# Two of four sums of transposed probabilities: formed by VectorE instead of GpSimd

## The chip, the cores and the metric

The kernel runs on one core of one Trainium2 chip. Five engines work side by side, each with its own queue of instructions, and meet through semaphores: TensorE (PE in the profile, with PEld for its weight loads), VectorE (DVE), ScalarE (ACT), GpSimd (POOL) and SyncE (SP, which here only issues DMAs). The metric is the time of one execution on the device, in microseconds (us). Lower is better. All data are float32.

## The reference

`x` has 8 batches of 100 rows of 512; `ctx` has 8 batches of 361 rows of 512. A small cross-attention with one head comes first, then a block with two cross-attentions of 16 heads of 128 over the same context, and an MLP:

```python
q, k, v = x @ w_q.T, ctx @ w_k.T, ctx @ w_v.T
x = x + alpha * (softmax(q @ k.T / sqrt(512)) @ v) @ w_o.T

for i in (1, 2):                       # two layers, 16 heads, K = 128
    h = layer_norm(x) * ln_scale + ln_offset
    qh, kh, vh = h @ wq + bq, ctx @ wk + bk, ctx @ wv + bv     # by head
    kh, vh = concat(kh, bias_k), concat(vh, bias_v)            # one more key: 362
    w = softmax(qh @ kh.T / sqrt(128))
    x = x + (w @ vh) @ wo + bo
h = layer_norm(x) * ln_scale + ln_offset
x = x + gelu(h @ w_fc1 + b_fc1) @ w_fc2 + b_fc2
```

## The kernel before

The 8 batches are taken in four pairs: `q` numbers the pair and `j` the batch within it (`QB` = 2). `l` is the layer. The 16 heads of 100 rows of a batch make 1600 rows, and these are cut into three groups `g` (`ROWS`: 576, 512 and 512 rows). A step is one `(l, q, g)`, so that there are 24 steps with two batches each, 48 rounds in all.

Instead of forming keys and values, the kernel multiplies each query by the transposed key weight (`queries`, `wide_queries`) and puts the result into the large tile `Z`. The scores are then `Z` times the context, and after the softmax the probabilities times the context go back into the same place in `Z` (`mixed`), from where `head_out` applies the value weight.

Both products are done with a scheme of seven block products instead of eight, in the manner of Strassen and Winograd. Such a scheme needs sums and differences of the blocks of both operands:

- For the scores, `pair_sums` (L700 to L703, GpSimd) forms four sums of blocks of `Z` for two tiles of 128 rows. `pair_part` runs the seven products in four parts. L752, L757 and L758 on VectorE add what comes out in PSUM. `pair_exps` takes the row maximum (L770, VectorE) and the exponential (L771, ScalarE), and `rows_normed` divides by the sum (L337 on VectorE, L338 on ScalarE). L751 on GpSimd writes the score of the extra key into the tile of probabilities, for which the transposes of that tile's former contents must be done.
- For the second product the probabilities must have the keys on the partitions. `rows_turned` calls `turned`, which transposes blocks of 32 by 32 on VectorE (L354), 16 instructions for a pair of tiles and 8 for the single tile of 64 rows in group 0. They go into `pT`, a tile of nine blocks: 0 to 5 hold the transposed probabilities, 6, 7 and 8 take sums. After the last transpose of a round `column_sums` writes one row to DRAM (L790, a DMA issued by SyncE) and forms four sums, L791 to L794. In the text L791 is the first sum (block 6), L792 the one that overwrites block 1, L793 the second (block 7) and L794 the last (block 8).
- `mixed` then runs the seven products with the context for each half `m` of the columns. Its part 0 needs block 6, part 1 needs block 7, part 2 the new block 1 and part 3 block 8. Its results are copied or added into `Z` by ScalarE (L836, L839, L844, L858) and VectorE (L847, L853, L854).

Other VectorE work that the text speaks of: L577 scales the transposed rows of a layer norm, L884 adds the bias of a head's output, L946 and its neighbours add up the output projection, L595 multiplies weights for the score of the extra key, L458 to L460 form sums of the transposed context in the first small attention, and L986 to L995 are sums of the same kind in the MLP.

The order of the units is written out by hand at the end of the program: `score_units` gives the parts of the scores of one round, and the products of the round before (`mix_units`), the projections of the next step and the output heads are woven between them. Within this order a planner of the framework gives each engine its own order, by rank: an instruction's rank is its place in the program, and the transposes get a rank 30 places later (`TURN_BEHIND`), so that they yield to other VectorE work. The four sums have the rank of their place.

`column_sums` has an argument for the engine, which is GpSimd unless `last_turned` calls it with VectorE. `score_units` reuses the name `n` before `end` reads it, so that `last_turned` is never built: in the profile all 48 rounds have their four sums on GpSimd.

Of the kernel before, what the change touches and what calls it, by code (L numbers as in the profile page):

```python
# [11 lines left out]
ALU = mybir.AluOpType  # L12
# [67 lines left out]
def two_cross_attentions(ctx: ExitStack, tc: tile.TileContext, a: dict, out: bass.AP):  # L80
    nc = tc.nc
# [696 lines left out]
    def columns(l, q, g, j):  # L778

        r0, r1 = ROWS[g]  # L780
        if (l, q, g, j) not in pTs:
            t = work.tile([P, 9 * GWIDTH // 2], F32, tag="pT", name=f"pT_{l}_{q}_{g}_{j}")
            pTs[l, q, g, j] = t[:, : 9 * (r1 - r0) // 2].rearrange("p (u n) -> p u n", u=9)
        return pTs[l, q, g, j][:, :6, :].rearrange("p (k h) n -> p k (h n)", k=3)

    def column_sums(l, q, g, j, engine=nc.gpsimd):


        t, t3 = pTs[l, q, g, j], columns(l, q, g, j)
        nc.sync.dma_start(out=pbd[l, q * QB + j][:, slice(*ROWS[g])], in_=t3[TS : TS + 1, 2, :])  # L790
        engine.tensor_tensor(t[:, 6], t[:, 1], t[:, 0], ALU.subtract)  # L791
        engine.tensor_tensor(t[:, 1], t[:, 1], t[:, 3], ALU.subtract)  # L792
        engine.tensor_tensor(t[:, 7], t[:, 3], t[:, 6], ALU.subtract)  # L793
        engine.tensor_tensor(t[:, 8], t[:, 2], t[:, 7], ALU.subtract)  # L794

    def rows_turned(l, q, g, j, r, quarter):

        p, dens, rows = probs[l, q, j, r]
        n = rows * len(dens)
        c0 = r - ROWS[g][0]  # L800
        turned(p, columns(l, q, g, j)[:, :, c0 : c0 + n], len(dens), rows, quarter)
        if r + n == ROWS[g][1] and quarter == 3:
            column_sums(l, q, g, j)

    def last_turned(l, q, g, j, r, m):

        p, _, rows = probs[l, q, j, r]
        c0 = r - ROWS[g][0] + m * P
        transposed(f"{l}_{q}_{r}_{m}", p[:, m, :], rows, columns(l, q, g, j)[:, :, c0 : c0 + rows])
        if m:  # L810
            column_sums(l, q, g, j, nc.vector)
# [520 lines left out]
```

## Time and profile before

| | |
|---|---|
| median of 3 runs | 2040.84 us (2040.75 to 2043.89) |
| the profiled execution | 2040.29 us, of which the span from the first to the last instruction is 2038.2 |
| mean granted TensorE clock | 0.995 |
| VectorE, busy | 1282.4 us |
| GpSimd, busy | 702.0 us |
| L354, the transposes on VectorE | 1664 instructions, 602.0 us |
| L791 to L794, on GpSimd | 48 each, median 0.73 us each |

The profile comes from one execution. "Busy" is the time in which an engine ran at least one instruction. A row of a group of instructions gives, after the bar, the busy time in us and the mean time of one in ns, then after the next bar the idle time of the engine just ahead of these instructions and, behind `<-`, what ended most of it. A row of the list of waits reads: the engine and its instruction, `<-` what it waited for, then the total, the number of waits and the longest. A line of the timeline has the start, the duration, the engine, the line, what is written and read and, in brackets, the idle time before it. TensorE takes two passes for a float32 product, so that each product shows as two instructions.

### The profile page before, as it was taken

The page shows a single profiled execution, that of the slowest core. Times are in us where ns is not written, and L with a number is a line of the kernel's source. Part 1 is how long each engine was busy: PE and PEld are TensorE (multiplying, and loading weights), DVE is VectorE, ACT ScalarE, POOL GpSimd, SP SyncE. Part 2 cuts the span into 40 slices and gives each one's busy share as a digit, 9 for nine tenths or more (in the row PEclk, how much of TensorE's full clock was granted, in tenths as well). Part 3 has the DMA queues.
Part 4 walks back from the last instruction along what each step waited for, and adds up shares of the span by engine and source line. Part 5 has one row for each costly group of instructions (what it writes and reads, how often), then busy time and mean ns, then how long its engine had stood idle before and what let it go on. Part 6 is the DMA issues. An engine that isn't in the chain of part 4 may idle for free.

```text
span 2038.2 us, 31454 instructions
## 1 busy us (share of the span) xinstructions
PE 1974.1 (97%) x10991; PEld 1801.1 (88%) x10991; DVE 1282.4 (63%) x3523; ACT 760.0 (37%) x2002; POOL 702.0 (34%) x1146
## 2 busy tenths in 40 slices
PE   9999999999999999999999999999999999989998
PEld 5668889998989889998999998989998998979998
DVE  2564766667666676666775766676767666765543
ACT  1324444444442343444432444444433444421231
POOL 3232432643344143534234322333243244225140
PEclk9999999999999999999999999999999999999999
DMA  8696224742645445534634453234244432135342
GB/s 256 251 322 191 83 81 135 217 134 78 191 133 153 131 138 176 181 97 128 207 113 131 114 184 103 87 93 156 87 124 123 145 115 82 56 97 164 111 129 74
DMA packets 250681, 283.87 MB, mean 139 GB/s; under 512 B 37608, under 2 KB 212108, under 8 KB 247196
## 3 DMA queue, kind: packets, MB, share of 16 engines
q1 hardware_dynamic: 246340, 271.51, 43.0%
q0 software_dynamic: 2112, 6.40, 0.9%
q10 hardware_dynamic: 2072, 3.97, 0.6%
q8 instruction: 87, 1.43, 0.3%
q14 instruction: 70, 0.57, 0.1%
HBM read 242.86 MB, written 38.97 MB: 138 GB/s over the span
## 4 chain that ended last, share of the span: by engine, by line
PE 73%; DVE 13%; DMA 5%; ACT 4%; POOL 3%; issue 2%; SPq 0%; DVEq 0%; POOLq 0%; ACTq 0%
PE sx L717 9%; PE mx L827 8%; PE mz L827 7%; PE pwo_P L940 7%; PE pq L657 7%; DVE pT L354 6%; PE po L877 6%; PE pqw L673 6%; PE sz L717 4%; PE my L827 3%; PE sy L717 2%; PE pfx L1080 2%; DMA xr<-xd 2%; PE sc L470 2%; PE pgx L1031 2%
## 5 line engine op out<-in xcount | busy, mean ns | idle before, releaser
L354 DVE STREAM_TRANSPOSE pT<-p 32x192 f32<-32x192 f32 (+1 forms) x1664 | 602.0, 362 | 84.6 <-ACT p L338 55.4
L827 PE MATMUL mx<-pT,ctx 128*128 128x256 f32 (+3 forms) x960 | 282.8, 393 | 21.1 <-ACT Z L836 6.2
L717 PE MATMUL sx<-cT,Z 128*128 128x181 f32 x1152 | 230.9, 319 | 5.6 <-DVE p L757 4.2
L751 POOL TENSOR_SCALAR p<-nsb 128x1 f32<-128x1 f32 x192 | 37.4, 214 | 532.7 <-DVE pT L354 490.2
L827 PE MATMUL mz<-pT,ctx 105*128 105x256 f32 (+3 forms) x768 | 209.3, 395 | 11.0 <-POOL pT L791 10.5
L717 PEld LDWEIGHTS sx<-cT,Z 128*128 128x128 f32 x1152 | 195.6, 191 | 20.1 <-DVE p L757 6.9
L827 PEld LDWEIGHTS mx<-pT,ctx 128*128 128x128 f32 (+1 forms) x960 | 169.2, 190 | 44.3 <-POOL pT L793 9.2
L877 PE MATMUL po<-Z,wv 128*128 128x200 f32 x1024 | 193.9, 333 | 0.8 <-DMA wv<-in_L_xattn_wv_dram 0.8
L673 PE MATMUL pqw<-q,wkT 128*128 128x200 f32 x1024 | 194.6, 332 | 0.0
L657 PE MATMUL pq<-hT,wq 128*128 128x200 f32 x1024 | 193.6, 333 | 0.0
L771 ACT ACTIVATE p<-p,nm 128x362 f32<-128x362 f32 x192 | 114.8, 598 | 190.0 <-DVE nm L770 187.6
L827 PEld LDWEIGHTS mz<-pT,ctx 128*128 128x128 f32 (+1 forms) x768 | 145.2, 192 | 43.5 <-POOL pT L791 14.7
L673 PEld LDWEIGHTS pqw<-q,wkT 128*128 128x128 f32 x1024 | 176.3, 190 | 5.4 <-issue 0.5
L877 PEld LDWEIGHTS po<-Z,wv 128*128 128x128 f32 x1024 | 175.0, 189 | 6.4 <-issue 1.3
L657 PEld LDWEIGHTS pq<-hT,wq 128*128 128x128 f32 x1024 | 175.0, 189 | 4.2 <-issue 1.4
L770 DVE TENSOR_REDUCE nm<-p 128x1 f32<-128x362 f32 x192 | 101.5, 529 | 103.1 <-ACT p L762 93.2
L717 PE MATMUL sz<-cT,sums 128*128 128x181 f32 x768 | 149.4, 316 | 1.1 <-ACT p L745 1.1
L700 POOL TENSOR_TENSOR sums<-Z 128x256 f32<-128x256 f32 x96 | 69.7, 726 | 233.3 <-ACT Z L676 158.6
L676 ACT COPY Z<-pqw 128x400 f32<-128x400 f32 x256 | 122.4, 490 | 68.5 <-PE pqw L673 68.4
L338 ACT ACTIVATE p<-p,rden 128x362 f32<-128x362 f32 (+2 forms) x216 | 129.0, 599 | 36.9 <-DVE rden L337 36.9
L717 PEld LDWEIGHTS sz<-cT,sums 128*128 128x128 f32 x768 | 124.7, 189 | 1.7 <-ACT p L745 1.6
L827 PE MATMUL my<-pT,ctx 128*128 128x256 f32 (+3 forms) x384 | 102.9, 389 | 0.0
(377 smaller groups left out, 3115.7 us busy)
## 6 DMA issues: line engine op xcount, KB each, us to landing
wv<-in_L_xattn_wv_dram SPq DMA_DIRECT2D x64, 512.0 KB
wq<-in_L_xattn_wq_dram SPq DMA_DIRECT2D x64, 512.0 KB
wkT<-wkd SPq DMA_DIRECT2D x48, 512.0 KB
cT<-cTd SPq DMA_DIRECT2D x16, 1267.0 KB
wo_S<-wod SPq DMA_DIRECT2D x32, 512.0 KB
f<-in_L_xattn_w_fc_dram SPq DMA_DIRECT2D x32, 512.0 KB
wo_A<-in_L_xattn_wo_dram SPq DMA_DIRECT2D x24, 512.0 KB
xr<-xd SPq DMA_DIRECT2D x46, 200.0 KB
```

The costliest lines, as they stand in the source:

```text
L338: nc.scalar.mul(p[:rows, :n], p[:rows, :n], rden[:rows])
L354: nc.vector.transpose(dst[keys, :, :, i, :], src[i * QD : (i + 1) * QD, :, :, quarter, :])
L657: nc.tensor.matmul(ps, w[:, c, (h % 2) * K : (h % 2 + 1) * K], hTs[l, q][:, c, :], start=(c == 0), stop=(c == DT - 1),)
L673: nc.tensor.matmul(ps[:, c, :], w[:, h % 2, cc * P : (cc + 1) * P], qs[h], start=True, stop=True)
L676: nc.scalar.copy(Z[:, 2 * c2 : 2 * c2 + 2, :, h * L : (h + 1) * L], ps.rearrange("p c (b t) -> p c b t", b=QB),)
L700: nc.gpsimd.tensor_tensor(t[:, 0], a2[:, :2, :], a2[:, 2:, :], ALU.add)
L717: nc.tensor.matmul(ps[:, :KH], st["a"][a][:, c, :], st["ct"][:, blk, c, :], start=(first and c == 0), stop=(c == 1), skip_group_check=not ...
L770: nc.vector.tensor_reduce(nm, p[:, :S1], AX.X, ALU.max, negate=True)
L771: nc.scalar.activation(p[:, :S1], p[:, :S1], AF.Exp, bias=nm, accum_out=den)
L827: nc.tensor.matmul(ps, cx[:w, blk, :], pT[:w, u, :], start=first, stop=last, skip_group_check=more)
L877: nc.tensor.matmul(ps, w[:, c, (h % 2) * K : (h % 2 + 1) * K], Z[:, c, :, h * L : (h + 1) * L], start=(c == 0), stop=(c == DT - 1),)
L940: nc.tensor.matmul(ps, w[:, h, :], OB[i, j][:, h, :], start=(h == 0 and not more), stop=(h == 7), skip_group_check=more)
```

## The change

The first and the third instruction of `column_sums`, L791 and L793, are issued to VectorE. L792 and L794 stay on the engine that is passed in, GpSimd in all 48 rounds. The operands, their shapes and the order in the program stay.

```diff
         t, t3 = pTs[l, q, g, j], columns(l, q, g, j)
         nc.sync.dma_start(out=pbd[l, q * QB + j][:, slice(*ROWS[g])], in_=t3[TS : TS + 1, 2, :])
-        engine.tensor_tensor(t[:, 6], t[:, 1], t[:, 0], ALU.subtract)
+        nc.vector.tensor_tensor(t[:, 6], t[:, 1], t[:, 0], ALU.subtract)
         engine.tensor_tensor(t[:, 1], t[:, 1], t[:, 3], ALU.subtract)
-        engine.tensor_tensor(t[:, 7], t[:, 3], t[:, 6], ALU.subtract)
+        nc.vector.tensor_tensor(t[:, 7], t[:, 3], t[:, 6], ALU.subtract)
         engine.tensor_tensor(t[:, 8], t[:, 2], t[:, 7], ALU.subtract)
```

The second sum reads the first, now on the same engine. L792 overwrites block 1, which the first sum reads, and L794 reads the second sum; both now follow VectorE.

## The prediction

> **What bounds the kernel now.** I read the page's busy shares first, then TensorE's waits in the attention part, then single places in the timeline.
>
> ```profile
> PE 1974.1 (97%) x10991; PEld 1801.1 (88%) x10991; DVE 1282.4 (63%) x3523; ACT 760.0 (37%) x2002; POOL 702.0 (34%) x1146
> ```
>
> TensorE works 97% of the span: with the work on it unchanged, only its idle 64 us can be won. By stage, it idles 14.5 us before 205 us, 38.9 between 205 and 1830 (the attention layers, where every column sum lies) and 10.7 in the MLP. Next I asked what ended the 38.9; the columns are the total, the number of waits and the longest, in us:
>
> ```profile
> PE mz L827 <- POOL pT L791: 10.5, 10, 2.3
> PE mx L827 <- ACT Z L836: 6.2, 4, 2.7
> PE mx L827 <- DVE Z L853: 5.1, 6, 2.1
> PE mx L827 <- POOL pT L793: 4.9, 6, 0.9
> PE sx L717 <- DVE p L757: 3.4, 4, 2.2
> ```
>
> The first and the fourth wait are on the two sums that move: together 15.4 us, 0.75% of the time and the ceiling of the direct gain. The second, third and fifth show the other side: TensorE also waits on evictions by ScalarE and VectorE, and VectorE gets more to do. One place shows the whole mechanism (start, duration):
>
> ```profile
> 495.31 0.75 DVE L354 STREAM_TRANSPOSE pT<-p 32x192 f32<-32x192 f32 x2
> ...
> 496.14 0.72 POOL L791 TENSOR_TENSOR pT<-pT 128x256 f32<-128x256 f32 x1 [0.91 <-DVE pT L354]
> ...
> 496.92 0.73 PEld L827 LDWEIGHTS mz<-pT,ctx 128*128 128x128 f32 x4 [1.22 <-POOL pT L791]
> 496.92 1.13 PE L827 MATMUL mz<-pT,ctx 128*128 128x256 f32 x4 [0.82 <-POOL pT L791]
> ...
> 498.19 0.72 POOL L793 TENSOR_TENSOR pT<-pT 128x256 f32<-128x256 f32 x1
> ...
> 498.97 0.70 PE L827 MATMUL mx<-pT,ctx 128*128 128x256 f32 x2 [0.91 <-POOL pT L793]
> ```
>
> The last transposes end at T = 496.06. GpSimd starts 0.08 later, takes 0.72, and TensorE goes on 0.06 after it, 0.86 after T. Then the queue holds a pair sum (L700) and L792 ahead of L793, so the second wait follows. In 35 of the 48 places the first sum waits directly for its transposes like this; in the other 13 GpSimd was still on other work.
>
> **Prices.** From the groups kept apart by shape:
>
> ```profile
> L854 DVE TENSOR_TENSOR Z<-my,Z 128x256 f32<-128x256 f32 x64 | 26.9, 421 | 1.9 <-PE my L827 0.4
> L791 POOL TENSOR_TENSOR pT<-pT 128x256 f32<-128x256 f32 x32 | 23.3, 729 | 55.9 <-DVE pT L354 29.2 <-issue 26.7
> L793 POOL TENSOR_TENSOR pT<-pT 128x256 f32<-128x256 f32 x32 | 23.2, 727 | 0.0
> ```
>
> No VectorE row has this size with both inputs in SBUF. L854 (one input in PSUM) gives 421 ns, and 446 at 288 columns; a line through 569 ns at 400 columns (L989) and 1222 at 1024 (L992 to L995) gives 418. I take 0.42 and 0.45.
>
> **What the Trainium skill says.** GPSIMD Engine Reference, section Elementwise — side-by-side cycle accounting: a two-input sum is about twice as fast on VectorE, mostly per element. Here it is 0.42 against 0.73. SBUF — State Buffer, section SBUF: two separate sides: a VectorE operation with two SBUF inputs and a GpSimd operation that reads SBUF take one port pair as an exclusive lock, whoever starts first. The trace agrees:
>
> ```profile
> 97.75 0.74 DVE L458 TENSOR_TENSOR cT_-1_4_631<-cT_-1_4_631 128x362 f32<-128x362 f32 x1
> 98.53 0.94 DVE L459 TENSOR_TENSOR cT_-1_4_631<-cT_-1_4_631 128x362 f32<-128x362 f32 x1
> 99.40 1.05 DVE L460 TENSOR_TENSOR cT_-1_4_631<-cT_-1_4_631 128x362 f32<-128x362 f32 x1
> ```
>
> Beside GpSimd's context sums L460 takes 1.05; elsewhere 0.53. Perfetto Trace Analysis, section Tensor Engine Instruction: VectorE and GpSimd run strictly in order, so what counts is where the planner puts the moved sums.
>
> **Part by part.**
>
> *Removed from GpSimd:* 2 x 48 sums, 23.3 + 14.3 + 23.2 + 12.7 = 73.5 us busy. GpSimd is 34% busy, so this pays nothing by itself; what pays is which result comes sooner.
>
> *Added to VectorE:* 32 x 2 x 0.42 + 16 x 2 x 0.45 = 41.3 us, to about 65%. Their rank in the order is the normal one, the transposes' is 30 lower, so the first sum should be next as soon as the last transpose is out, and the second behind it. No new wait on VectorE for another engine: the first sum reads only what VectorE wrote, the second also the first (some 0.07 for the hand-over; L993 starts about that long after L992).
>
> *First sum ready:* T + 0.03 + 0.42 + 0.06 = T + 0.51, not T + 0.86. In the ten waits: at 298.5, 496.9, 927.8 and 1352.4 (0.82, 0.82, 1.03, 0.82) 0.35 each is won, 1.40; at 239.9 (0.55, 288 columns) 0.40; at 1817.3 (2.34) 0.41; at 722.7 (1.09), where GpSimd came 0.37 after T, 0.64; at 210.9, 833.5 and 1729.8 (1.03, 0.35, 1.69) GpSimd was busy with L700 to L703 for 0.8 to 2.6 us past T, and the whole wait goes, 3.07. Sum 5.9.
>
> *Second sum ready:* T + 0.94, or T + 1.67 behind one GpSimd operation holding the lock. In the place shown TensorE would want it at about T + 1.63, so all six waits go: 4.9. Gross gain 10.8.
>
> *Third and fourth sum stay on GpSimd:* L792 must not overwrite what the first sum reads, so GpSimd now waits for VectorE there, until T + 0.53, where it used to wait for the transposes until T + 0.08. Behind it are L794, L751 and the pair sums L700 to L703. But two operations of 0.73 have left the queue: L792 ends near T + 1.3 to 1.7 and L794 near T + 2.0 to 2.4; before, 2.2 and 3.0 without other work between. No wait of TensorE on either was recorded, and I expect none.
>
> *VectorE's hold:* 0.94 us in 48 places, 1.67 with one lock wait, 2.3 with two. What is queued behind: L752, L757, L758, L946, L577, L884 or the next softmax. For each place I subtracted VectorE's idle gaps before the next L757 or L853 and that one's slack to the matmul that waits for it (mostly 1.4 to 2.7). A hold of 0.94 then delays TensorE once, by 0.9 (at 760.4, slack 0.05); 1.67 costs 2.2 in four places; 2.3 costs 8.2 in twelve. At 760.4 VectorE is itself locked out by GpSimd's column sums, which become fewer, so 0.9 may vanish. I take 1.5; the bounds are 0 and 8.2. The scores' own chain (maximum, exponential, reciprocal, transposes) is covered by gaps of 0.8 to 2.3 us within the next few instructions.
>
> *DMA and queues:* nothing is moved. L790, issued by SyncE, reads the transposes and stays in front; no DMA is issued by VectorE or GpSimd here.
>
> *Given back:* TensorE arrives earlier at later waits. The ones on L836, L853 and L757 hang on engines that TensorE itself feeds and shift along; those on DMAs don't. I take 1.4 of the 10.8, a choice.
>
> Sum: 10.8 - 1.5 - 1.4 = 7.9. Profiled execution: 2038.2 span + 2.1 around it = 2040.3; the median is 2040.8, 0.5 above. So about 2032.4 for a profiled run and **2033 us** for the median. About 0.2%, 4 us, is what a measurement can tell from no change.
>
> **The rivals.**
>
> *The lock makes VectorE late (slower).* GpSimd wakes from L751 on the same transposes and starts L700 or L792 just then. If both new sums regularly wait a whole 0.73, the hold is 2.3 and costs 8.2; the first sum comes at T + 1.24, 0.4 later than now in seven of the ten waits (2.7 lost; 3.1 still won in the other three), and of the second's 4.9 about 2.5 remain. Net 8.2 + 2.7 - 3.1 - 2.5 = 5.3 slower: 2046. For it: the doubled L460, and L988 at 1.66 for 0.57. Against it: in 35 places GpSimd is idle until T, so VectorE starts first. It decides from a hold of about 1.8 us up, where the slacks of 1.4 to 1.8 are used up.
>
> *The gain is given back.* If what follows each removed wait is bound elsewhere (L836 and L853 come right after in the same product), three quarters are lost: 2.7 - 1.5, about 1 us faster, 2040. For it: 17% of the chain that ended last runs over VectorE and ScalarE. Against it: TensorE has only 39 us of idle left there.
>
> *Deeper gain.* With 73 us off GpSimd the pair sums come earlier, L595 meets fewer locks, and part of the waits on L853 and L836 goes as well: 5 more, and 2027.
>
> *The sums don't sit behind their block.* If the planner places them behind an eviction that waits for TensorE (L752 and L946 stand idle up to 2.3 us there), the first sum comes 1.5 to 3 us late in some places: up to 6 slower, 2047. The ranks speak against it.
>
> **How the numbers follow.** Chances: the forecast 0.55 (2029 to 2037), deeper 0.13, given back 0.15, lock 0.12, misplaced 0.05. Faster by over 0.2%: nearly all of the forecast, the deeper case and a little of the third, 0.67; within: most of given back and the forecast's edge, 0.16; slower 0.17. The range reaches from the deeper case to the lock: 2026 to 2045.
>
> **What would show it.** Right: waits of TensorE on L791 near 4.6 us, now under VectorE; those on L793 gone; L791 and L793 on VectorE at 0.42 to 0.6 mean; VectorE busy near 1325, GpSimd near 630; TensorE's idle in 205 to 1830 near 31. Wrong: means near 0.9 on VectorE (lock), or waits on L757, L853 and L836 grown by as much as those on L791 and L793 shrank.

## The result, and the profile after

| | before | after |
|---|---|---|
| median of five runs each | 2040.75 us (2038.72 to 2043.89) | 2048.60 us (2048.44 to 2051.75) |
| ratio | 1 | 1.0036, 95% interval 1.0021 to 1.005 |
| profiled execution, and its span | 2040.29, 2038.2 us | 2051.75, 2049.8 us |

The change makes the kernel slower, by 7.8 us in the medians and 7.3 by the ratio. The prediction, 2033 and a range of 2026 to 2045, missed the sign. The profiled execution of after is the longest of its five, 3.2 us above the next, so its page shows 11.6 us of span where the medians show 7.8.

The page's line of busy shares, after:

```profile
PE 1977.6 (96%) x10991; PEld 1806.6 (88%) x10991; DVE 1326.4 (65%) x3619; ACT 758.2 (37%) x2002; POOL 640.8 (31%) x1050
```

The work went where it was to go: VectorE has 44 us more, GpSimd 61 less. Of the 11.6 us of span TensorE's idle time has 8.1 (2049.8 - 1977.6 against 2038.2 - 1974.1) and its busy time, for the same instructions, 3.5. TensorE idles 14.2 us before 205 us (14.5 in before), 47.1 between 205 and 1840 (39.7) and 10.9 behind that (9.9), so most of what was added lies in the attention layers. Next, what TensorE waited for (total, number of waits, longest, in us):

```profile
PE mz L827 <- DVE pT L791: 8.9, 8, 2.3
PE mz L827 <- ACT Z L839: 6.8, 7, 1.3
PE mx L827 <- ACT Z L836: 6.1, 4, 2.7
PE sz L717 <- ACT p L745: 5.9, 6, 1.5
PE sx L717 <- DVE p L757: 5.1, 9, 1.5
PE mx L827 <- DVE Z L853: 4.1, 6, 1.3
PE sx L717 <- ACT p L742: 3.9, 5, 1.4
```

The waits on L793 are gone (4.9 before) and those on L791 fell from 10.5 to 8.9. Two rows that were next to nothing have come up instead. In before they were:

```profile
PE sz L717 <- ACT p L745: 1.1, 2, 0.7
PE mz L827 <- ACT Z L839: 0.4, 1, 0.4
```

Both are copies out of PSUM by ScalarE, which nobody edited. L742, a third such copy, rose from 2.6 too. L757 was 4.2 in the whole run of before. One wait of 2.0 us, at 579 us, stands under GpSimd's L607 in this profile, but it is most likely L853's: the same product of before waits 2.15 for L853, and in after L853 and L607 end within 0.02 us of each other. With it L853 has 6.1, where it had 5.1.

One place shows how. The timeline of before, around the probabilities of the lone 64-row tile (start, duration):

```profile
398.90 0.15 DVE L337 RECIPROCAL rden<-den 64x1 f32<-64x1 f32 x1
...
399.09 0.60 ACT L338 ACTIVATE p<-p,rden 64x362 f32<-64x362 f32 x1 [0.22 <-DVE rden L337]
...
399.78 0.30 ACT L745 COPY p<-sz 128x180 f32<-128x180 f32 x1
...
400.66 0.78 PE L717 MATMUL sz<-cT,sums 128*128 128x181 f32 x4
```

The same place after:

```profile
398.48 0.78 PE L717 MATMUL sz<-cT,sums 128*128 128x181 f32 x4
...
399.70 0.67 DVE L791 TENSOR_TENSOR pT<-pT 128x288 f32<-128x288 f32 x1
...
400.63 0.64 DVE L793 TENSOR_TENSOR pT<-pT 128x288 f32<-128x288 f32 x1
...
401.19 0.15 DVE L337 RECIPROCAL rden<-den 64x1 f32<-64x1 f32 x1
401.37 0.60 ACT L338 ACTIVATE p<-p,rden 64x362 f32<-64x362 f32 x1 [1.51 <-DVE rden L337]
...
401.87 0.29 ACT L745 COPY p<-sz 128x180 f32<-128x180 f32 x1
...
402.21 0.88 PE L717 MATMUL sz<-cT,sums 128*128 128x181 f32 x4 [0.99 <-ACT p L745]
```

The two sums, with L884 (0.41) between them, sit ahead of the reciprocal L337 on VectorE. ScalarE has nothing to do with the sums, but its queue has the division L338 next and stands for 1.51 us (0.22 before). The copy L745 needs neither: its product ended at 399.26. It is only queued behind L338. And the copy frees the PSUM tile that TensorE's next product accumulates in, so TensorE stands for 0.99. The division itself is in no hurry, as e9 and e10 will show. The second form, at 469 us after, has the sums ahead of the row maximum L770, ScalarE's exponential L771 waiting for it, and the copy L839 behind:

```profile
469.73 0.91 DVE L793 TENSOR_TENSOR pT<-pT 128x256 f32<-128x256 f32 x1
...
471.52 0.53 DVE L770 TENSOR_REDUCE nm<-p 128x1 f32<-128x362 f32 x1
...
472.14 0.60 ACT L771 ACTIVATE p<-p,nm 128x362 f32<-128x362 f32 x1 [1.07 <-DVE nm L770]
...
472.74 0.35 ACT L839 COPY Z<-mz 128x256 f32<-128x256 f32 x1
...
473.14 1.13 PE L827 MATMUL mz<-pT,ctx 128*128 128x256 f32 x4 [0.87 <-ACT Z L839]
```

In the same place of before L771 waited 0.20 and TensorE not at all:

```profile
469.61 0.60 ACT L771 ACTIVATE p<-p,nm 128x362 f32<-128x362 f32 x1 [0.20 <-DVE nm L770]
...
470.21 0.35 ACT L839 COPY Z<-mz 128x256 f32<-128x256 f32 x1
...
470.64 1.11 PE L827 MATMUL mz<-pT,ctx 128*128 128x256 f32 x4
```

### The profile page after: what moved, and what is told of

It reads as the page before. It is cut to its first block, busy times and chain, and to the rows that moved or that the text cites. A ratio compares the mean times of both kernels' runs of the same rounds, so it can differ in the third digit from the quotient of the medians.

```text
span 2049.8 us, 31449 instructions
## 1 busy us (share of the span) xinstructions
PE 1977.6 (96%) x10991; PEld 1806.6 (88%) x10991; DVE 1326.4 (65%) x3619; ACT 758.2 (37%) x2002; POOL 640.8 (31%) x1050
## 4 chain that ended last, share of the span: by engine, by line
PE 71%; DVE 17%; DMA 5%; ACT 4%; issue 2%; POOL 1%; SPq 0%; DVEq 0%; ACTq 0%; POOLq 0%
DVE pT L354 8%; PE sx L717 8%; PE mx L827 8%; PE pwo_P L940 7%; PE mz L827 7%; PE pq L657 7%; PE pqw L673 6%; PE po L877 5%; PE sz L717 4%; PE my L827 3%; PE sy L717 2%; PE sc L470 2%; PE pfx L1080 2%; PE pgx L1031 1%; DMA xr<-xd 1%
## 5 line engine op out<-in xcount | busy, mean ns | idle before, releaser
L771 ACT ACTIVATE p<-p,nm 128x362 f32<-128x362 f32 x192 | 114.8, 598 | 197.6 <-DVE nm L770 195.2
L770 DVE TENSOR_REDUCE nm<-p 128x1 f32<-128x362 f32 x192 | 101.5, 529 | 102.7 <-ACT p L762 93.4
L338 ACT ACTIVATE p<-p,rden 128x362 f32<-128x362 f32 (+2 forms) x216 | 129.1, 599 | 41.4 <-DVE rden L337 41.4
```

Source lines behind the costliest of these rows:

```text
L338: nc.scalar.mul(p[:rows, :n], p[:rows, :n], rden[:rows])
L770: nc.vector.tensor_reduce(nm, p[:, :S1], AX.X, ALU.max, negate=True)
L771: nc.scalar.activation(p[:, :S1], p[:, :S1], AF.Exp, bias=nm, accum_out=den)
```

## The experiments

Two theories. **The queue of ScalarE** (theory A): what VectorE's hold costs, it costs through copies that stand in ScalarE's in-order queue behind an operation waiting for VectorE. **The lock** (theory B in the first four): sums on VectorE and GpSimd's own sums lock each other out of SBUF, and the stretched sums are the loss. Where an expectation has a third theory, it states it; that of e1 and e2, theory C, is that the planner's changed order is the loss. From e9 on theory B is that VectorE's lateness reaches TensorE in whatever order ScalarE works. "Before" was run with each group of experiments; its median there was 2042.2, 2042.2 and 2041.1, so ratios are compared across groups, and times within one. The groups are e1 to e6, e8 to e11 and e12 to e14.

| run | ratio to before, 95% interval | median, us |
|---|---|---|
| e1, first sum alone on VectorE | 1.0007 (0.9998 to 1.0017) | 2042.8 |
| e2, second sum alone on VectorE | 1.0055 (1.004 to 1.0069) | 2052.6 |
| e4, VectorE held, sums on GpSimd | 1.0033 (1.0021 to 1.0044) | 2047.7 |
| e6, division traced later | 1.003 (1.0019 to 1.0041) | 2048.0 |
| e9, after, division behind the copies | 0.9989 (0.9981 to 0.9998) | 2039.8 |
| e10, e9 and exponential behind the copy | 0.9942 (0.9924 to 0.9959) | 2030.6 |
| e11, e10's queue, sums on GpSimd | 0.9974 (0.9962 to 0.9985) | 2036.7 |
| e8, before, L793 ahead of L792 | 0.9976 (0.9965 to 0.9987) | 2037.1 |
| e12, e10 with the pair sums behind L792 | 0.9949 (0.9929 to 0.9969) | 2031.4 |
| e13, e11 and e8 together | 0.9949 (0.993 to 0.9968) | 2029.8 |
| e14, e11 with VectorE held | 0.9981 (0.9972 to 0.999) | 2037.6 |

**e1 and e2: one sum at a time.**

```diff
 e1:  t[:, 6]  nc.vector     t[:, 7]  engine
 e2:  t[:, 6]  engine        t[:, 7]  nc.vector
```

> Only the first sum (L791) on VectorE, the other three on GpSimd. Theory A (the length of VectorE's hold: the sums run ahead of the reciprocal L337, the evictions and the maximum L770; ScalarE stands in order on L338 or L771 for them, and its copies L745 and L839, for which TensorE waits, come late): about half the hold of the changed kernel, so half of its new waits on L745, L839 and L757 (14 us in the changed kernel, about 4 in the kernel before), with a little of the wait on L791 won: 2041 to 2045 us. Theory B (the port lock between VectorE and GpSimd is what costs): one sum meets the lock only with the pair sums, 2041 to 2043, and L791 on VectorE stays above 0.5 us on average. Theory C (the loss is in the planner's changed order, not in the hold): as slow as the changed kernel, 2048.

> Only the second sum (L793) on VectorE, behind GpSimd's first. Theory A: half the hold, and the planner can put the sum behind other VectorE work, because it is not ready right behind the transposes; but where it is next in VectorE's order it must wait for GpSimd, which lengthens the hold to 0.7 us and more. The wait on L793 (4.9 us) goes, the one on L791 (10.5) stays. 2040 to 2046 us. Theory B: the second sum meets GpSimd's L792 every time and the lock costs the same as in the changed kernel, 2046 to 2049. Theory C: 2048.

e1 measured no difference that can be told from zero: the wait on L791 fell by 1.7 us (10.5 to 8.8), and those on L745 and L839 rose from 1.5 to 5.7. It lies in the ranges of A and B alike; against C it is 5 us too fast. e2 was the slowest of all, and slower than any theory had it. The reason is in the profile of e2's L793, whose columns are the engine's idle time before it and how often:

```profile
L793 DVE TENSOR_TENSOR pT<-pT x48: 424/457/964, 211.4 to 1836.2; 128x256 f32<-128x256 f32 x32, 128x288 f32<-128x288 f32 x16
its engine sat idle before it (us, times) until:
  POOL pT L791: 43.6, 46
```

VectorE stood 0.95 us (43.6 / 46) for GpSimd's first sum in nearly every round, and then worked 0.55 on average. So its hold was 1.5 us, the longest of the series, although it does one sum only. TensorE's waits on ScalarE's copies L742, L745 and L839 together are about twice as long with the two long holds as with the two short ones (e4 is the next experiment):

| | mean hold of VectorE per round, us | L742 + L745 + L839 |
|---|---|---|
| before | 0 | 4.1 us |
| e1 | 0.56 | 8.7 |
| e4 | 0.77 | 8.4 |
| after | 1.3 (0.88 to 2.1, once 4.2) | 16.6 |
| e2 | 1.5 | 17.1 |

**e4: the hold alone.** All four sums on GpSimd, and two row maxima of 0.42 and 0.41 us into a scratch tile on VectorE in the place of the sums. They have one SBUF input each, took 0.40 to 0.45 us in all 48 rounds, so that nothing stretched them, and hold VectorE for 0.77 us.

```diff
+        hold = small.tile([P, 2], F32, tag="hold", name=f"hold_{l}_{q}_{g}_{j}")
+        nc.vector.tensor_reduce(hold[:, :1], t[:, 3], AX.X, ALU.max)
+        nc.vector.tensor_reduce(hold[:, 1:], t[:, 5], AX.X, ALU.max)
```

> All four sums on GpSimd as before; behind each block VectorE runs two row maxima over blocks 3 and 5 of the transposed probabilities, whose results nobody reads. One input each, so that no port lock can arise, about 0.42 to 0.46 us each: the hold of the change without its sums. Theory A: TensorE's waits on L791 and L793 stay (15 us) and those on L745, L839, L742 and L757 grow by some 8 to 10 us: 2048 to 2052 us. Theory B (lock): no lock, so within 3 us of the kernel before, 2040 to 2044.

The loss is there without the sums and without their lock. It lies just under theory A's range and well above theory B's. In the profile L742, L745 and the shifted L839 (L840) have 8.4 us of waits, so about 4.3 of the 9.6 us by which its span is longer; 5.2 is TensorE's busy time, which the last section takes up. L757 fell by 1.0, so the waits that theory A named grew by 3.3, not by 8 to 10.

**e6: the division traced later.** In `score_units` of the changed kernel, the late units of the lone tile follow part 0 instead of preceding it.

```diff
-                    u, late = late[:n] + u, late[n:]
+                    first = g == 0 and m == 0 and part == 0
+                    u, late = u + late[:n] if first else late[:n] + u, late[n:]
```

> The changed kernel with one unit moved: the softmax division of the single tile of 64 rows (L337, L338) comes behind part 0 of the next pair instead of ahead of it, so that ScalarE's copies L742 and L745 stand ahead of L338 in its queue. Theory A: TensorE's waits on L745 (5.9 us, six of about 1) go, those on L839 (6.8) stay: 2042 to 2045 us. Theory B or C: ScalarE's order is not where the time is, 2047 to 2050.

A miss that says nothing on either theory: the planner put L338 ahead of L745 again in five of the six places. In the one that it turned, at 208 us, the wait of 0.70 went. The place in the program alone doesn't set the order on ScalarE; an order edge does. As e6 is nearly the changed kernel, its 1.003 also repeats the loss, in 13 more runs.

**e9 and e10: the copies first.** Both keep VectorE's sums. e9 adds to e6 an edge that queues the lone tile's division behind L745 (L746 there). e10 also holds back the exponential, where the part 0 of a mixed product is traced directly behind it, and queues it behind that part's last copy, L839. An edge orders the issue on ScalarE and adds no wait for another engine.

```diff
+            with tc.issue_after(copied[l, q, j, PAIRS[0][0]].ins):     # e9, rows_normed
+                normalise(f"{l}_{q}_{j}_{r}_{m}", p[:, m, :], dens[m], rows, S1)
...
-        nc.scalar.activation(p[:, :S1], p[:, :S1], AF.Exp, bias=nm, accum_out=den)
+        pending.append(lambda: nc.scalar.activation(p[:, :S1], p[:, :S1], AF.Exp, bias=nm, accum_out=den))
...
-            nc.scalar.copy(c22, z)                                     # e10, mixed, part 0
+            out = nc.scalar.copy(c22, z)
+            with tc.issue_after(out.ins):
+                flush()
```

> The changed kernel with ScalarE's division of the lone tile's probabilities (L338) put behind ScalarE's two copies of the next pair's first products (L742, L745 of the changed kernel) by an order edge, in all 16 places; VectorE and GpSimd keep the four sums as changed. Theory A (the loss is a copy standing in ScalarE's in-order queue behind an operation that waits for VectorE): the waits of TensorE on L745, 5.9 us, fall under 1.5, the ones on L839 (6.8) stay, and the kernel takes 2042 to 2045. Theory B (VectorE's work is late and TensorE meets the delay anyway, a little further on): the waits move to the transposes or L757, 2047 to 2050.

> The one before this, and also the exponential of a score block (L771) put behind ScalarE's copy of the first mixed product (L839) where the exponential was traced directly ahead of that product, 22 places. Theory A: the waits on L839 (6.8 us) go as well, under 1.5, and the kernel takes 2036 to 2041, less than before. Theory B: the exponential's lateness returns as waits on transposes or on L757, 2046 to 2050.

Theory A holds, and more was won than it said: by the ratios, some 10 us against after with the first edge and 19 with both, uncertain by 3 and 5. TensorE's waits in e10, in whose numbering L806 is L791, L851 is L836, L871 is L853, L768 is L757, L862 is L844 and L753 is L742:

```profile
PE mz L842 <- DVE pT L806: 8.9, 8, 2.3
PE mx L842 <- ACT Z L851: 6.2, 4, 2.7
PE mx L842 <- DVE Z L871: 5.5, 7, 2.1
PE sx L728 <- DVE p L768: 5.0, 8, 2.0
...
PE mx L842 <- ACT Z L862: 3.8, 3, 2.1
...
PE sx L728 <- ACT p L753: 2.7, 4, 0.9
```

The rows of L745 and L839 are no longer in the list. The sums hold VectorE as long as in after, 1.31 us on average from the start of the first to the end of the second, and the place shown above tells what differs. Theory C falls here too: VectorE's order is nearly that of after, L902 (L884 there) between the two sums included, and the loss is gone. In e10's timeline L808 is L793, and L342 and L343 are L337 and L338:

```profile
395.59 0.67 DVE L806 TENSOR_TENSOR pT<-pT 128x288 f32<-128x288 f32 x1
395.65 0.30 ACT L756 COPY p<-sz 128x180 f32<-128x180 f32 x1
...
396.52 0.64 DVE L808 TENSOR_TENSOR pT<-pT 128x288 f32<-128x288 f32 x1
396.95 0.78 PE L728 MATMUL sz<-cT,sums 128*128 128x181 f32 x4
397.08 0.15 DVE L342 RECIPROCAL rden<-den 64x1 f32<-64x1 f32 x1
397.26 0.60 ACT L343 ACTIVATE p<-p,rden 64x362 f32<-64x362 f32 x1 [1.31 <-DVE rden L342]
```

The sums are as long (0.67, 0.64), the division still waits 1.31, but the copy (L756) is through ahead of it and TensorE takes its product without a wait.

**e11: the control.** Both edges of e10, with all four sums back on GpSimd.

> Control: both order edits of ScalarE's queue in the kernel before, with all four sums on GpSimd. Theory A: there the operations that stood ahead of the copies had hardly waited (TensorE's waits on L745 and L839 were 1.1 and 0.4 us), so little is to be won: 2038 to 2042, within 2 us of before. Theory B says the same, 2039 to 2042. If instead it gains 4 or more, the order of ScalarE's queue is a loss of its own and says little on the change.

It won 5.5 us, over the 4 that its expectation named: the order on ScalarE was a loss of its own. TensorE's waits on L745 and L839 in before were only 1.5 of it; where the rest came from was not followed up. By the ratios, of the 19 us between after and e10 some 5 are due to the order in any case and 14 to the two together. The pair to read is e10 against e11, of one group: with the copies first, the same two sums on VectorE make the kernel 6.1 us faster (2030.6 against 2036.7, uncertain by some 4), where with the old order they made it 7.8 slower.

**e14: the hold again.** e4's two row maxima added to e11.

> The row maxima of e4, which only hold VectorE behind each column (four sums on GpSimd), together with ScalarE's reordered queue (e11). Theory A (the hold of VectorE costs only through ScalarE's queue): 2035 to 2039, within 2 us of e11 (2036.7), where the same hold cost 5.6 to 7 with the old queue. Theory B (VectorE's hold costs TensorE by VectorE's own lateness): 2041 to 2045, with waits on L757 and on transposes grown.

Theory A: 0.9981 against 0.9974, 1.4 us with an uncertainty of some 3, where the same hold cost 6.7 with the old order. This hold of 0.77 us costs nothing that can be told from zero once no copy stands behind what waits for it.

**e8 and e13: no VectorE at all.** In `column_sums` of before (e8), or of e11 (e13), only the order on GpSimd changes.

```diff
+        engine.tensor_tensor(t[:, 7], t[:, 3], t[:, 6], ALU.subtract)
         engine.tensor_tensor(t[:, 1], t[:, 1], t[:, 3], ALU.subtract)
-        engine.tensor_tensor(t[:, 7], t[:, 3], t[:, 6], ALU.subtract)
```

> The kernel before with only the order of two sums on GpSimd exchanged: the one of L793 is put ahead of the one of L792, so that the two sums TensorE asks for first come first. VectorE and ScalarE keep their order. Theory A (the change loses because VectorE's two sums push ScalarE's queue): nothing is pushed here, so the waits on the second sum (4.9 us before) fall to under 1.5 and the kernel takes 2036 to 2039. Theory B (what is won on the second sum is given back at the next wait, whatever forms it): waits on evictions grow by as much, 2040 to 2042. A third, slower: the sum that is now third comes late for its product and TensorE waits for it, over 2043.

> All four sums on GpSimd with L793 ahead of L792 (e8), and ScalarE's queue reordered (e11). Theory A (the two edits act on different waits and add up): e8 won 5.1 and e11 won 5.5, so 2030 to 2033, as fast as VectorE's two sums with the same queue (2030.6). Rival (both win the same waits): 2035 to 2037.

In e8 the sum of block 7, now on line 792, comes one GpSimd operation earlier and TensorE's waits on it are 1.2 us instead of 4.9. The time falls by 5.1 us, so none of the 3.7 is given back. With the copies first, both gains add up: 2029.8 is level with e10 and, like it, clearly below both kernels. By the ratios against e11, the new order on GpSimd (e13) wins some 5 us and the move to VectorE (e10) some 6.5: most of what the change could win needed no other engine.

**e12: the lock.** e10, with GpSimd's pair sums queued behind L792 of the last traced column (the "third" of the edit), which waits for the first sum. This keeps them off the first sum only; the second can still meet GpSimd's work.

```diff
+        if thirds:
+            with tc.issue_after(thirds[0].ins):
+                sums_of(l, q, j, r)
...
```

> The changed kernel with ScalarE's queue reordered (e10), and GpSimd's pair sums (L700 to L703 of the changed kernel) put behind the third sum of the last traced column, so that none of them runs while VectorE forms the first sum. Theory A (the wait on the first sum shrank by 1.6 us only, from 10.5 to 8.9, because a pair sum on GpSimd holds the lock in five of the eight places and VectorE's sum takes 0.90 to 0.97 instead of 0.42): the sum takes 0.42 to 0.45 there and the waits on it fall to about 6; the kernel takes 2026 to 2029. Rival: the pair sums come late for their own products and TensorE waits for GpSimd there: 2032 to 2036, with waits on sums of GpSimd over 4 us.

Half right. The same place of e10, then of e12 (L816 is L791, L817 is L792):

```profile
492.05 0.73 POOL L706 TENSOR_TENSOR sums<-sums,Z 128x256 f32<-128x256 f32 x1
492.15 0.90 DVE L806 TENSOR_TENSOR pT<-pT 128x256 f32<-128x256 f32 x1
...
493.20 1.10 PE L842 MATMUL mz<-pT,ctx 128*128 128x256 f32 x4 [1.04 <-DVE pT L806]
```

```profile
492.48 0.42 DVE L816 TENSOR_TENSOR pT<-pT 128x256 f32<-128x256 f32 x1
492.99 0.73 POOL L817 TENSOR_TENSOR pT<-pT 128x256 f32<-128x256 f32 x1 [1.33 <-DVE pT L816]
493.05 1.10 PE L854 MATMUL mz<-pT,ctx 128*128 128x256 f32 x4 [0.56 <-DVE pT L816]
```

In e10 a pair sum, L706 (L701 in after), starts 0.10 ahead of VectorE's sum and this one takes 0.90. In e12 GpSimd is idle, the sum takes 0.42, and the wait falls from 1.04 to 0.56. Over 48 rounds the first sum takes more than 0.6 us once, against 14 times in e10. So GpSimd's sum is what stretches VectorE's, shown by taking it away. That agrees with the lock that the Trainium skill (SBUF — State Buffer, section SBUF: two separate sides) states. Whether VectorE stands until GpSimd has wholly ended, the runs don't show: in e10 only 0.27 passes from the recorded end of L706 to that of the sum, less than the 0.42 of a sum alone. All told the waits on the first sum fell from 8.9 to 6.2, as expected. But the time stayed at 2031.4: TensorE's waits on VectorE's additions (L757 and L853 in after) rose.

```profile
PE mx L854 <- DVE Z L883: 7.6, 8, 2.1
PE sx L738 <- DVE p L778: 7.5, 9, 2.5
PE mz L854 <- DVE pT L816: 6.2, 7, 2.3
```

They have 4.6 us more than in e10 (5.5 and 5.0 there). The rival's waits on pair sums didn't come. The additions themselves are not stretched (at most 0.35 and 0.46 us, as in e10), so they start later; what holds them up stays open.

## Why the prediction was wrong

**The direct gain of 10.8 was over-sized; it is 6.5.** The waits on L793 went entirely, as predicted (4.9). The waits on L791 were to lose 5.9 and lost 1.6. "In 35 places GpSimd is idle until T, so VectorE starts first" was read off the trace of before, where GpSimd is idle because its next instruction is L791, waiting for the transposes. With L791 gone from its queue, it runs the next pair sum just then:

```profile
498.52 0.72 POOL L701 TENSOR_TENSOR sums<-sums,Z 128x256 f32<-128x256 f32 x1
498.62 0.91 DVE L791 TENSOR_TENSOR pT<-pT 128x256 f32<-128x256 f32 x1
...
499.67 1.10 PE L827 MATMUL mz<-pT,ctx 128*128 128x256 f32 x4 [1.04 <-DVE pT L791]
```

This is the place of the prediction, where TensorE waited 0.82 before. It waits 1.04 now, and in five of the eight places left the first sum takes 0.90 to 0.97.

**VectorE's hold, taken at a cost of 1.5, is the step that failed.** The hold itself was 1.31 us on average (median 1.03) and not 0.94: the two sums took 1.19 together, stretched as in the place above, and in 18 rounds other VectorE work stood between them. But the cost was mis-sized for two other reasons. The slack was counted only at L757 and L853, VectorE's own results for TensorE. And "The scores' own chain (maximum, exponential, reciprocal, transposes) is covered by gaps of 0.8 to 2.3 us" is true of that chain, as e10 shows, but ScalarE's queue hangs on it: each of its waits for L337 and L770 also delays the copies behind, for which TensorE leaves little slack: in the two places of before, 0.6 us from the end of L745 to the product that needs it and 0.1 from that of L839. Against before, TensorE's waits grew by 6.4 on L839, 4.8 on L745, 1.3 on L742, 1.0 on L853, 0.9 on L757 and 0.7 on L844. That is 15.1 where 1.5 was set, 12.5 of it on the three copies, and it exceeds even the upper bound of 8.2. Against it stand 6.5 won on the sums; the difference, 8.6, is about the 8.1 by which TensorE's idle time grew. None of the prediction's signs of being wrong came: the sums took 0.55 and 0.65 on average, not 0.9, and L757, L853 and L836 together grew by 1.8 us, not by the 6.5 that the sums won. Most of the loss stood at waits that it didn't name.

**The rivals.** Two of them were slower, at 2046 and 2047, near the 2048.6 by luck. The lock's mechanism is real, but it is not the loss: its waits on L757, and on the sums, are not what grew, and e4 loses as much without it. It costs part of the gain and lengthens the hold. The case that the sums don't sit behind their block fell: the first sum follows the last transposes within 0.04 us in five of the eight places where TensorE still waits for it, and within 0.43 in the others. In all 48 rounds it does so 40 times.

**The rest stood.** VectorE was to be near 1325 busy (1326.4) and GpSimd near 630 (640.8), and no wait of TensorE on L792 or L794 came up. "Given back", 1.4, can't be told from nothing: where the queue doesn't interfere, e10 against e11 won 6.1, uncertain by 4, and their waits on the two sums differ by 6.9 (10.9 + 4.9 in e11, 8.9 in e10). TensorE's idle time between 205 and 1830, which was to fall from 38.9 to 31, rose instead: up to 1840 it is 39.7 in before, 47.1 in after and 33.7 in e10.

## What to carry to other kernels

When work is put onto an engine, follow not only its own results to the bound engine but every in-order queue that waits for it, and list what stands behind each waiting instruction: that the waiting instruction itself has slack says nothing on those. "The other engine is idle then" has to be read from its queue without the moved instruction, since an in-order engine that waits for it looks idle. And before an operation moves to a faster engine, try a better place for it in the queue that it is in.

## What was not expected of the hardware

TensorE's busy time, for the same instructions, differs by run: 1974.1 us before, 1977.6 after, 1979.3 in e4, 1967.1 in e13. In some stretches of 3.4 us the granted clock is one half. One of after, which begins at 580 us behind a stall (the columns after each engine's busy time end with the granted clock, the DMA share and GB/s):

```profile
576.00:580.00 4.00, 1.98 (x10) 1.54 (x9) 2.27 (x10) 2.81 (x8) 3.03 (x7) 1.00 0.57 163
580.00:583.40 3.40, 3.40 (x13) 3.37 (x12) 3.02 (x9) 1.24 (x4) 0.72 (x1) 0.53 0.13 45
583.40:587.00 3.60, 3.60 (x20) 3.41 (x20) 3.25 (x9) 1.88 (x5) 0.54 (x2) 0.97 0.38 116
```

In the 4 us ahead of it TensorE worked for 1.98, and its longest standstill was 2.02. That standstill is the wait for L853 at 579 us. Ahead of the end of the span, before has five such stretches (at 118, 708, 930, 1818 and 1883 us), after seven (two of them in a row at 133), e13 three. At half speed each costs about 1.7 us, so two more make 3.4 of the 3.5 us of busy time that after has over before. One of the two lies before 205 us, where nothing was changed. The Trainium skill (TensorE: Matmul & The Clock Gate, section Part 1: The HAM clock gate (the "warmup" mystery)) has the clock at one half after an idle window of about 3.4 us; here a half-idle one went ahead of it. It doesn't bring the half clock each time: in the same place of before TensorE worked for 1.85 of the 4 us from 573.7, with a standstill of 2.15, and the clock stayed whole behind it. Where a stall does bring it, the stall costs more than its length. So the same stall brought it in one execution and not in the other; how many of these stretches a kernel gets by its stalls and how many by chance, the runs don't settle.

The clock is not the loss, though. The granted clock, averaged over the runs of each kernel, is 0.9948 in after and 0.9942, 0.9943 and 0.9945 in the three groups of before; e2, the slowest, has 0.9953. Nor is it the same everywhere: e10 has 0.9960 and e11 0.9945. Over some 1970 us of busy time that is an estimate of 3 us, so up to half of the 6.1 between these two can lie in the clock; of the 19 between after and e10 it is some 2.
